# Four-layer graph network on one core: one more head's score sum on VectorE, one fewer on ScalarE, in the third layer

## The chip, the cores and the metric

The kernel runs on one core of one Trainium2 chip. The metric is the time of one execution on the device in microseconds; a version's time is the median of its runs.

## The reference

A graph has 3125 nodes with 64 features each and 103125 edges, sorted by destination (50000 drawn edges in both directions and one self loop per node). Four graph layers follow one another, each on `relu(layernorm(x))`, and each result is added to `x`: a mean aggregation (L0, two steps), a stochastic convolution (L1, two steps), a GATv2 attention with five heads (L2, two steps and a dense layer), and a relational attention (L3, two steps). Only L2 matters here. One step of it is

```
xl = (x @ Wl + bl).reshape(n, H, C);  xr = (x @ Wr + br).reshape(n, H, C)     # H = 5, C = 64
e = leaky_relu(xl[src] + xr[dst], 0.2)
alpha = einsum('ehc,hc->eh', e, att)                  # one score for each edge and head
a = exp(alpha - segment_max(alpha, dst)[dst])
out = segment_sum(a / denom[dst] * xl[src], dst)      # then the mean over heads, and a bias
```

In L2 the reference adds a self loop for each node to the edges.

## The kernel before, in words

The 103125 edges are cut into 806 tiles of 128 edges, one edge on each partition. In L2 a chunk is 18 tiles (`CT2`), so that there are 45 chunks a step, and the two steps (the loop over `l` at line 958, called "layers" of the stage below) go through all of them one after the other. Tiles are scored in pairs: 403 pairs a step, 806 in the stage.

Every table row holds 66 numbers for each head: the 64 features and two columns with 0.2 times the attention product and its negative. With these the leaky ReLU's score becomes a plain sum over 66 numbers of `max(v, 0) * weight`. For one pair `score` (line 968) does this:

- POOL gathers the source rows of 6 tiles at a time into a buffer `g` (line 976, helper at line 257; nine such buffers).
- PE makes the destination rows of each tile by a matmul of a 0/1 matrix with a window of the table (line 983), into one of two PSUM tiles `px`.
- VectorE adds both (line 984) and applies maximum and weight (line 986), in place in `g`.
- The sums over 66 numbers give the scores `al`. `ACT_HEADS = 4` (line 862) divides them: VectorE sums the first `H - ACT_HEADS` heads of both tiles by one reduction (line 987). ScalarE sums each other head of each tile by a copy activation into a scratch tile `junk` with an accumulated output (line 991). In the profile each of these is an ACTIVATE and an ACTIVATION_READ_ACCUMULATOR.
- `top` (line 1000), called in the next pair's `score`, takes on VectorE the maximum of `al` and the self loop's score, into `am`. It needs all five sums of the pair.

The steps for a whole chunk, `weigh_turn` to `nodes`, are issued between pairs a fixed number of pairs after the chunk's last one (the list at line 1097, carried out by `attend`, line 1102): transposes of `am` on PE, scans on VectorE for the maximum of each destination, the exponential on ScalarE (line 1017), weights on VectorE (lines 1029 to 1032), the sums on PE (helper at line 254), copies from PSUM on ScalarE (lines 1047 and 1058), and the nodes' new rows. In the first step the nodes' rows are also multiplied out and stored for the second (`row_steps`, lines 904 to 945). A buffer `g` comes free when its sums on PE are done.

The text above gives the program's order. The order on each engine is drawn up when the program is built, by a planner with its own costs: of what it expects to be ready it takes the earliest of the program. Each engine then runs its list in order and waits on semaphores. Only a few instructions are pinned to the program's order (`tc.keep_in_program_order`: register loads and line 852 in L2); lines 984 to 1000 are not among them. SP issues the direct transfers, POOL the gathers.

Of the kernel before, what the change touches and what calls it, by code (L numbers as in the profile page):

```python
# [63 lines left out]
def bcast(ap, axis, n):  # L64
    shape = list(ap.shape)
    shape.insert(axis, n)
    return ap.unsqueeze(axis).to_broadcast(shape)
# [73 lines left out]
def sorted_path(ctx: ExitStack, tc: tile.TileContext, A: dict, out: bass.AP):  # L141
# [712 lines left out]
    def layer2(y_prev):  # L854
# [4 lines left out]
        GW = SW + D + 1  # L859
        MS = D + 1 + H  # L860
        GT = 6
        ACT_HEADS = 4
        t_l = [tables[f"l2_{l}l"] for l in range(2)]
        t_r = [tables[f"l2_{l}r"] for l in range(2)]
        y = tables["l2_y"]
        with tc.tile_pool(name="l2", bufs=1) as lp, tc.tile_pool(name="l2_s", bufs=2) as sp, \
# [91 lines left out]
            for l in range(2):  # L958
# [9 lines left out]
                def score(s, i):  # L968
# [15 lines left out]
                    nc.vector.tensor_add(g[:, :, :SW], g[:, :, :SW], px[:, :, :SW])  # L984
                    HV = H - ACT_HEADS
                    nc.vector.scalar_tensor_tensor(g[:, :, :F], g[:, :, :F], 0.0, bcast(att08[l], 1, 2), op0=OP.max, op1=OP.mult)  # L986
# [356 lines left out]

    y1 = spmm_layers()
    y2 = layer2(y1)
    y3 = layer3(y2)
    with tc.tile_pool(name="fin", bufs=1) as fp:
# [662 lines left out]
```

## Time and profile before

| | |
|---|---|
| median of 11 runs | 9907.65 us (9843.82 to 9937.45) |
| the profiled execution: its own time, its span | 9917.3 us, 9915.4 us |
| busy in the span: PE, DVE, ACT, POOL | 4455.0, 4240.1, 2481.6, 4957.7 us |
| L2: first and last start of line 984 | 4093.9 and 7269.8 us |
| line 984, 986, 987 on DVE (806 each), mean of one | 842, 834, 278 ns |
| line 991 on ACT (6448), mean of ACTIVATE, of the accumulator's read | 247, 187 ns |
| gathers of L2 on POOL (806 in each step), mean of one | 1116, 1100 ns |

DVE is VectorE, ACT is ScalarE, PE is TensorE, POOL is GpSimd, SP is SyncE. A row of waits reads: engine, tile and line that stood idle, what released it, the idle time in us, how often, and the longest. A row of a group ends with the busy time and the mean of one in ns, and the idle time ahead of it. A row of the timeline starts with the start and the duration in us; the idle time ahead of the instruction stands in brackets. Releasers are inferred from semaphores: "issue" means that nothing visible was waited for, "remote" an unknown queue. Both instructions of a sum on ScalarE overlap the next one's, so that their durations add up to more than the engine's busy time.

### The profile page before, as it was taken

To read this page: it belongs to the slowest core of one execution; us is meant where nothing else is said; L and a number is where in the kernel's file an instruction comes from. 1 tells how busy PE (TensorE), PEld (TensorE's weight loads), DVE (VectorE), ACT (ScalarE), POOL (GpSimd) and SP (SyncE) were. 2 spreads that over 40 slices of the span, in tenths; PEclk is the share of its full clock that TensorE was granted. 3 is DMA by queue.
4 is the path that set the end of the run, shared out by engine and by line. 5 is a ranking of instruction groups with operands and counts; after the bars stand their busy time and mean duration, and the time that the engine had idled before them with its cause. 6 is when DMAs were issued, how large, how long until landed. Compare 5 with 4: busy or idle time off the path is not lost. (4 is left out here: it accounts for less than half of the span.)

```text
span 9915.4 us, 104742 instructions
## 1 busy us (share of the span) xinstructions
PE 4455.0 (45%) x23937; PEld 3412.8 (34%) x23937; DVE 4240.1 (43%) x12144; ACT 2481.6 (25%) x15657; POOL 4957.7 (50%) x4849
## 2 busy tenths in 40 slices
PE   5996995322222223355555434444452333422222
PEld 5995994222222222122222212222232222312222
DVE  5762111212212223577777757666642333323333
ACT  2331000000000000366666546555530000100000
POOL 0000003666666665255656455555526666566665
PEclk8996555555655666555555555555555555555555
DMA  2332332111111121344454344444421222111111
GB/s 70 125 118 80 136 131 67 46 47 46 47 43 46 46 50 43 119 128 134 136 137 137 108 123 123 127 119 127 121 68 37 42 41 42 40 32 35 35 35 35
DMA packets 542968, 799.05 MB, mean 81 GB/s; under 512 B 253426, under 2 KB 386153, under 8 KB 530315
## 3 DMA queue, kind: packets, MB, share of 16 engines
q0 software_dynamic: 206464, 439.52, 18.4%
q1 hardware_dynamic: 335883, 352.72, 11.3%
q8 instruction: 209, 3.42, 0.2%
q14 instruction: 412, 3.38, 0.1%
HBM read 657.39 MB, written 134.39 MB: 80 GB/s over the span
## 5 line engine op out<-in xcount | busy, mean ns | idle before, releaser
L257 POOL DMA_INDIRECT g<-l,idx x1616 | 1568.2, 970 | 2330.2 <-issue 2022.3
L991 ACT ACTIVATE junk<-g 128x66 f32<-128x66 f32 x6448 | 1573.9, 247 | 877.5 <-ACT junk L991 375.1
L257 POOL DMA_INDIRECT g<-l_0l,src_t x806 | 899.3, 1116 | 786.9 <-PE px L983 257.6
L257 POOL DMA_INDIRECT g<-l_1l,src_t x806 | 886.8, 1100 | 746.8 <-PE acc L254 404.5
L991 ACT ACTIVATION_READ_ACCUMULATOR junk<-g 128x1 f32 x6448 | 1207.3, 187 | 0.2
L257 POOL DMA_INDIRECT g<-l_0v,idx x806 | 795.0, 986 | 575.3 <-issue 216.7
L257 POOL DMA_INDIRECT g<-l_1v,idx x806 | 806.4, 1001 | 436.5 <-issue 232.9
L537 PE MATMUL acc<-hit,g 128*128 128x128 f32 x3232 | 624.3, 355 | 815.7 <-issue 476.4
L983 PE MATMUL px<-win,oT 36*128 36x335 bf16 x1612 | 569.5, 461 | 646.4 <-DVE g L984 439.1
L537 PEld LDWEIGHTS acc<-hit,g 128*128 128x128 f32 x3232 | 561.5, 260 | 863.0 <-issue 510.3
L984 DVE TENSOR_TENSOR g<-g,px 128x670 f32<-128x670 f32 x806 | 667.7, 842 | 373.5 <-remote 178.1
L612 PE MATMUL pv<-h_l,a 128*128 128x64 f32 x4700 | 800.9, 347 | 15.8 <-ACT a L605 13.4
L612 PEld LDWEIGHTS pv<-h_l,a 128*128 128x128 f32 x4700 | 792.2, 262 | 43.8 <-ACT a L605 28.3
L986 DVE SCALAR_TENSOR_TENSOR g<-g,att 128x660 f32<-128x660 f32 x806 | 670.5, 834 | 0.0
L254 PE MATMUL acc<-ao,g 128*70 128x72 f32 x3224 | 444.2, 329 | 276.4 <-DVE ao L1032 159.6
L254 PEld LDWEIGHTS acc<-ao,g 128*70 128x70 f32 x3224 | 401.0, 236 | 405.2 <-DVE ao L1032 239.3
L540 ACT COPY sums<-acc 128x128 f32<-128x128 f32 x68 | 18.1, 266 | 2056.6 <-remote 1413.3
L254 PE MATMUL acc<-oh,g 128*68 128x12 f32 x3224 | 400.2, 268 | 210.2 <-issue 102.6
L245 DVE TENSOR_TENSOR sums<-sums,carry 128x1 f32<-128x1 f32 (+2 forms) x166 | 26.0, 157 | 1079.0 <-issue 718.6
L822 PE MATMUL pm<-ident,mx 90*128 90x90 f32 (+2 forms) x158 | 65.3, 413 | 932.1 <-DVE mx L820 621.9
L1257 ACT COPY qm<-px 128x128 f32<-128x128 f32 x404 | 104.5, 267 | 1469.4 <-remote 787.2
L254 PEld LDWEIGHTS acc<-oh,g 128*68 128x68 f32 x3224 | 382.0, 230 | 249.8 <-issue 122.7
(327 smaller groups left out, 7505.9 us busy)
## 6 DMA issues: line engine op xcount, KB each, us to landing
a_d<-a SPq DMA_DIRECT2D x47, 1600.0 KB
a<-a_d SPq DMA_DIRECT2D x47, 1600.0 KB
g<-l,idx POOLq DMA_INDIRECT x1616
ea<-in_edge_attr_dram SPq DMA_DIRECT2D x33, 768.0 KB
ea<-in_edge_attr_n_dram SPq DMA_DIRECT2D x33, 768.0 KB
oT<-dl_d SPq DMA_DIRECT2D x88, 162.0 KB
oT<-dl_d SPq DMA_DIRECT2D x66, 216.0 KB
g<-l_0l,src_t POOLq DMA_INDIRECT x806
```

What stands on the lines that cost most here:

```text
L245: return tc.keep_in_program_order(op(*args, **kwargs))
L254: nc.tensor.matmul(acc[..., bass.ds(at, width)], lhsT, rhs, start=False, stop=True, skip_group_check=True)
L257: nc.gpsimd.indirect_dma_start(out=to, out_offset=None, in_=table, in_offset=bass.IndirectOffsetOnAxis(ap=idx, axis=0))
L537: nc.tensor.matmul(st["acc"][:M], g[:, k, :], h[:, k, :], start=(i == 0 and k == 0), stop=(end and k == 3))
L540: nc.scalar.copy(st["sums"][:M], st["acc"][:M])
L612: nc.tensor.matmul(st["pv"][:, :D], st["a"][:, b], h_l[l][:, b], start=(b == 0), stop=(b == NBK - 1))
L822: nc.tensor.transpose(s["pm"][:, :R], m[:R], ident[:R, :R])
L983: nc.tensor.matmul(px[:, j, :SW], s["oT"][:, q * P:(q + 1) * P], s["win"][:, i, :], start=True, stop=True)
L984: nc.vector.tensor_add(g[:, :, :SW], g[:, :, :SW], px[:, :, :SW])
L986: nc.vector.scalar_tensor_tensor(g[:, :, :F], g[:, :, :F], 0.0, bcast(att08[l], 1, 2), op0=OP.max, op1=OP.mult)
L991: nc.scalar.activation(junk, g[:, j, hd * C2:(hd + 1) * C2], AF.Copy, accum_out=al[:, q0 + j, hd:hd + 1])
L1257: nc.scalar.copy(qm[:, :m].rearrange("p k h r -> p (k h r)"), px[:, :m * H * R])
```

## The change

`ACT_HEADS` goes from 4 to 3. `HV` in `score` becomes 2, and with it line 987 reduces 128 x (2 tiles, 2 heads, 66) in place of 128 x (2 tiles, 1 head, 66), and the loop at line 989 issues three activations for each tile in place of four, six for a pair in place of eight. Nothing else of the source changes; the planner draws up the order anew.

```
         MS = D + 1 + H
         GT = 6
-        ACT_HEADS = 4
+        ACT_HEADS = 3
         t_l = [tables[f"l2_{l}l"] for l in range(2)]
...
                    HV = H - ACT_HEADS
                    nc.vector.scalar_tensor_tensor(g[:, :, :F], g[:, :, :F], 0.0, bcast(att08[l], 1, 2), op0=OP.max, op1=OP.mult)
                    nc.vector.tensor_reduce(al[:, q0:q0 + 2, :HV], g[:, :, :HV * C2].rearrange("p k (h c) -> p k h c", h=HV), AX.X, OP.add)
                    for j in range(2):
                        for hd in range(HV, H):
                            junk = sp.tile([P, C2], F32, name="junk")
                            nc.scalar.activation(junk, g[:, j, hd * C2:(hd + 1) * C2], AF.Copy,
                                                 accum_out=al[:, q0 + j, hd:hd + 1])
```

More of the change, by code (lines that the diff above doesn't have):

```diff
@@ L861, in layer2 @@
         GT = 6
-        ACT_HEADS = 4
+        ACT_HEADS = 3
         t_l = [tables[f"l2_{l}l"] for l in range(2)]
```

## The prediction

> **What bounds the kernel now.** I read the page's busy line and its 40 slices first, to see that no engine is full over the whole span, and then only the stage that the change touches. Line 984 runs in that stage alone, from 4093.9 to 7269.8 us in the view of that line: 3176 us, 806 pairs of tiles, 3.94 us a pair. The busy time by stretch, one row for each of the two layers of the stage (PE, weight loads, DVE, ACT, POOL), says:
>
> ```profile
> 4090.00:5665.00 1575.00, 763.22 (x3458) 428.71 (x3458) 1171.15 (x3206) 946.96 (x6755) 893.29 (x802) 0.52 0.48 130
> 5700.00:7250.00 1550.00, 683.31 (x3226) 393.88 (x3226) 1014.50 (x2751) 883.45 (x6440) 873.76 (x793) 0.51 0.45 123
> ```
>
> VectorE is the busiest, 74% and 65%, and nobody is full. The first layer also prepares the rows of the next one, which costs VectorE 157 us more, and yet both layers take nearly the same time. So VectorE's sum of work is not what sets the pace. The waits of VectorE in the stage say what does:
>
> ```profile
> DVE am L1000 <- ACT junk L991: 396.9, 174, 9.5
> DVE g L984 <- remote: 178.1, 19, 16.8
> DVE am L1000 <- remote: 104.0, 15, 20.0
> DVE g L984 <- PE px L983: 97.9, 64, 2.7
> DVE g L984 <- issue: 53.3, 30, 7.9
> DVE am L1000 <- issue: 44.8, 15, 20.7
> ```
>
> The largest one is line 1000, the maximum over the scores, waiting for ScalarE's sums of line 991. Going through all 806 of them, 221 sit behind a gap of more than 0.1 us, 572 us together. The reader should compare that with the load: ScalarE is busy 60% of the time, so it is late, not full. Why it is late shows in the order of time; here are one of these waits and ScalarE's activations ahead of it:
>
> ```profile
> 6199.19 0.26 ACT L991 ACTIVATE junk<-g 128x66 f32<-128x66 f32 x1 [1.08 <-ACT junk L991]
> 6200.62 0.26 ACT L991 ACTIVATE junk<-g 128x66 f32<-128x66 f32 x1 [1.08 <-ACT junk L991]
> 6202.04 0.26 ACT L991 ACTIVATE junk<-g 128x66 f32<-128x66 f32 x1 [1.06 <-ACT junk L991]
> 6203.46 0.26 ACT L991 ACTIVATE junk<-g 128x66 f32<-128x66 f32 x1 [1.07 <-ACT junk L991]
> 6204.89 0.26 ACT L991 ACTIVATE junk<-g 128x66 f32<-128x66 f32 x1 [1.07 <-issue]
> 6206.97 0.26 ACT L991 ACTIVATE junk<-g 128x66 f32<-128x66 f32 x1 [1.74 <-remote]
> 6207.69 0.26 ACT L991 ACTIVATE junk<-g 128x66 f32<-128x66 f32 x1 [0.37 <-ACT junk L991]
> 6207.95 0.24 ACT L991 ACTIVATE junk<-g 128x66 f32<-128x66 f32 x1
> 6208.19 0.24 ACT L991 ACTIVATE junk<-g 128x66 f32<-128x66 f32 x1
> ...
> 6207.69 0.17 DVE L1000 TENSOR_TENSOR am<-al,g 128x10 f32<-128x10 f32 x1 [8.84 <-ACT junk L991]
> ```
>
> Undisturbed, an activation with its read of the accumulator starts every 0.24 us (the last rows). In stretches it starts only every 1.42 us, though it has its data. Such stretches lie where POOL has been sending gathers back to back; ScalarE runs at full pace when POOL pauses. The eight activations of a pair take 1.70 us from the first start to the last in the median; 131 of the 806 groups take over 3 us, 742 us together. I don't know what slows them; what matters here is that the price is paid per activation.
>
> **The change, part by part.** *Removed:* two of eight activations per pair, with their accumulator reads. At 0.24 us start to start that is 0.48 us a pair, 806 x 0.48 = 387 us of ScalarE. Where ScalarE is undisturbed this is worth almost nothing by itself: VectorE has 2.8 us of other work per pair beside it (2236 us busy from 4090 to 7300, over 806). It is worth something where line 1000 waits. For each of the 221 waits I took the start times of its eight activations. If the last two drop out and the others keep their times, the wait gets shorter by the time from the sixth start to the eighth, at most by the whole wait: 256 us together. If instead a quarter of the group's length goes, again at most the wait, it is 217 us. I take 217, because the activations that leave are the fourth and the eighth, not the last two.
>
> *Added:* line 987 sums 264 elements in place of 132. The rows near it:
>
> ```profile
> L987 DVE TENSOR_REDUCE al<-g 128x2 f32<-128x132 f32 x288 | 77.9, 279 | 0.0
> L936 DVE TENSOR_REDUCE xr<-es 85x5 f32<-85x330 f32 x32 | 15.5, 485 | 0.0
> L1073 DVE TENSOR_REDUCE hn<-num 85x64 f32<-85x320 f32 x32 | 21.3, 665 | 0.0
> ```
>
> Lines 987 and 936 read along the row: (485 - 279) / (330 - 132) = 1.04 ns an element, so 132 more elements cost 0.138 us, 111 us over 806 pairs. Line 1073 reads across heads, 2.1 ns an element; by it the sum would be up to 0.27 us a pair, 220 us, the upper end. The new sum reads along the row, so I take 0.138. In the 221 pairs that wait at line 1000 the longer sum runs inside the wait, since ScalarE's activations need line 986 and not line 987; that leaves 585 x 0.138 = 81 us. The lower end is nothing, by the two layers above: 157 us more of VectorE's work did not lengthen a layer, and the addition is 55 us a layer.
>
> *Neither adds nor moves:* transfers. The gathers, the window loads and the register loads on SP are the same. POOL waits for ScalarE's reads of the gathered buffers (152 us in its waits), and would get buffers no later; the gather of a pair ends some 30 us before line 984 reads it (the pair at 4638.5 us was gathered by 4596.5), so that is cover enough for a late buffer. PE's line 983 waits 439 us for line 984 to free one of two banks; the 0.14 us reaches PE there, and comes back to line 984 only where PE is late, 98 us in line 984's waits. No wait is added; what gets done earlier is what stands behind the activations on ScalarE, its copies for PE (lines 1047, 1058), and no transfer hangs on those alone.
>
> *Sum:* 81 - 217 = -136 us if the slow stretches shrink with the number of activations. But the stretches follow POOL's gathers, whose number stays. If the 742 us stay as they are, groups of six pass through them faster: 131 x 8 / 6 = 175 pairs in place of 131, 44 more. A pair outside costs (3176 - 742) / 675 = 3.61 us, so that is 44 x 3.61 = 159 us gained, less 81: -78 us. I take -85, near the second, because ScalarE's pace follows the gathers in the rows. The profiled execution took 9917.3 us (span 9915.4), 9.65 us above the median of the 11 runs, so the sum is carried to the median: 9907.65 - 85 = 9823 us.
>
> A rule against this: the Trainium skill, Perfetto Trace Analysis, section Identifying the Most-Contended Engine, says to find the engine with the highest occupancy and to improve that one first. By it VectorE is the engine to relieve, the change loads it further, and the time would rise by up to the whole 111 us, to 10019. The wait rows say that the busiest engine stands still for the less busy one, and the comparison of the layers agrees with the rows; so I go by them.
>
> **The rivals.**
> *VectorE is on the path after all (slower).* In the undisturbed stretches VectorE's instructions follow one another without a gap, and any addition there goes to the end. If the time lost in the slow stretches does not fall (ScalarE's lateness then being a matter of the stretch alone, with the same 572 us of waits), the change costs 81 to 111 us: 9989 to 10019. For it: the first layer has the more work and the fewer long gaps. Against it: the equal length of the layers, and waits that end with a particular activation. It decides if less than 81 us of the 572 disappear.
> *The order is drawn up anew and line 1000 comes earlier (slower).* No wait pins line 1000 among VectorE's instructions; it stands where the planner expects ScalarE to be done. With six activations it can move ahead of one more of the long steps, line 984 or 986, 0.84 us each. In an undisturbed stretch that costs nothing; at a wait, that step no longer runs before it. 221 x 0.84 = 186 us at most, against the 136 gained: +50, 9958. It decides from 162 waits that lose a step. Against it: the gap in the order between lines 986 and 987 of the next pair, where line 1000 often stands now, is already early.
> *The gain is taken elsewhere (no change).* The long gaps at line 984 (178 us, 19 times, in the second layer nearly all) can grow by what those at line 1000 lose, as POOL waits 405 us in that layer for PE's sums (line 254) to free buffers. Then the first layer gains its half of the 85, and the second only pays its half of the 81: 9907.65 - 42 + 41 = 9906.
>
> **How the numbers follow.** Within 0.3% (30 us) is about what a measurement can't tell from no change. The forecast, faster by more than that: 0.50; it spans from 9690 (256 gained at line 1000 and a quarter of the 178 at line 984, 81 paid) to 9875. No change: 0.13. VectorE on the path: 0.19. Order: 0.18. So faster 0.50, same 0.13, slower 0.37. The range of 9690 to 10005 leaves out about one in ten on each side: a costlier sum or both slower cases together above, a collapse of the slow stretches below.
>
> **What would show it.** Right: line 987 at about 416 ns over 264 elements, 806 times; line 991 at 4836, still 0.24 us apart when undisturbed; line 1000's gaps 100 to 220 us below 572; the last start of line 984 some 85 us earlier against the first; VectorE's busy time 111 us up. Wrong: the gaps at line 1000 as long as before (first rival), more but shorter gaps there with line 984 now behind them (second), or growing gaps at line 984 and in POOL's waits for PE (third). What would make it wrong most simply is that the pace of the activations in the slow stretches depends on how many there are, in either direction.

## The result and the profile after

The changed kernel takes 10156.3 us (median of 12 runs, 10138 to 10197) against 9892.8 us (46 runs of the kernel before): ratio 1.0269, 95% interval 1.0252 to 1.0286. It is slower by 263 us, where 85 us less had been predicted. Its profiled execution took 10160.05 us with a span of 10158.3 us.

By the first and last start of line 984, the stage of L2 splits like this:

| us | before | after | difference |
|---|---|---|---|
| first step of L2 | 1553.4 | 1832.9 | +279.5 |
| between the steps | 42.7 | 43.1 | +0.4 |
| second step of L2 | 1579.9 | 1535.9 | -44.0 |
| after the last line 984 | 2645.6 | 2657.2 | +11.6 |

One step of L2 gained 44 us, and the other lost 280. Here is the busy time of the two steps after the change (columns as in the prediction: PE, weight loads, DVE, ACT, POOL):

```profile
4090.00:5940.00 1850.00, 797.27 (x3454) 440.07 (x3455) 1222.18 (x3206) 743.84 (x5143) 845.58 (x798) 0.50 0.41 111
5965.00:7500.00 1535.00, 689.45 (x3301) 392.82 (x3300) 1119.43 (x2813) 704.95 (x4978) 855.31 (x801) 0.51 0.46 125
```

In the first step nobody works much more than before, and VectorE is now busy 66% of it instead of 74%. So the loss is waiting. The groups of lines 991, 987 and 1000 in the stage say that the instructions themselves came out as predicted (busy time, mean ns of one, idle time ahead):

```profile
L991 ACT ACTIVATE junk<-g 128x66 f32<-128x66 f32 x4836 | 1183.8, 247 | 1179.1 <-issue 604.8 <-ACT junk L991 318.7 <-remote 176.9
L987 DVE TENSOR_REDUCE al<-g 128x4 f32<-128x264 f32 x806 | 328.7, 417 | 0.0
L1000 DVE TENSOR_TENSOR am<-al,g 128x10 f32<-128x10 f32 x806 | 135.0, 167 | 366.9 <-ACT junk L991 267.0 <-remote 71.0 <-issue 23.4
```

The wait at line 1000 shrank, 572 to 367 us, but in the first step alone: counting gaps of more than 0.1 us, it went from 283 to 73 us there, and from 288 to 290 in the second. The waits of VectorE in the stage show what took its place, and those of ScalarE where it comes from:

```profile
DVE am L1000 <- ACT junk L991: 267.0, 158, 6.4
DVE g L984 <- PE px L983: 248.7, 95, 12.8
DVE g L984 <- remote: 178.6, 35, 13.9
DVE g L984 <- PE pt L810: 143.1, 16, 10.8
```

```profile
ACT junk L991 <- issue: 604.8, 324, 11.3
ACT junk L991 <- ACT junk L991: 318.7, 502, 1.6
ACT sums L1047 <- remote: 224.2, 50, 13.3
ACT u L1058 <- remote: 204.7, 30, 8.7
```

VectorE now stands ahead of line 984. Counted in the same way, the gaps there went from 116 to 554 us in the first step. That rise of 437 us, less the 210 at line 1000, plus the 51 us by which VectorE's work grew, is 278 of the step's 279.5. In the second step the gaps at line 984 went the other way, 257 to 129 us; that is where its gain comes from. And ScalarE has two new waits that end with nothing visible: the copy `sums` (line 1047) and the copy `u` (line 1058). The next rows are one chunk's end in the first step, ScalarE, PE and VectorE in three fences (start, duration, and idle time in brackets):

```profile
5581.49 0.58 ACT L1047 COPY sums<-acc 70x510 f32<-70x510 f32 x1 [2.63 <-remote]
5588.66 0.43 ACT L1058 COPY u<-px 85x330 f32<-85x330 f32 x1 [6.59 <-remote]
```

```profile
5582.13 1.70 PE L1055 MATMUL px<-wh,sums 70*85 70x65 f32 x10 [2.46 <-issue]
5583.62 0.39 PE L1056 MATMUL px<-wsel,sums 70*85 70x5 f32 x2
5583.94 0.74 PE L983 MATMUL px<-win,oT 36*128 36x335 bf16 x2
...
5589.15 0.72 PE L983 MATMUL px<-win,oT 36*128 36x335 bf16 x2 [3.90 <-ACT u L1058]
```

```profile
5581.96 0.22 DVE L1138 COPY am<-am 128x5 f32<-128x5 f32 x1
5590.77 0.85 DVE L984 TENSOR_TENSOR g<-g,px 128x670 f32<-128x670 f32 x1 [8.59 <-PE pt L810]
...
5595.70 0.85 DVE L984 TENSOR_TENSOR g<-g,px 128x670 f32<-128x670 f32 x1 [3.99 <-remote]
```

PE has `px` ready for the copy at 5584.01 (5583.62 + 0.39). ScalarE has nothing else to do and starts the copy at 5588.66, 4.65 us late. `u` is read from one of the two `px` tiles, so PE's line 983 at 5589.15 waits for it. VectorE stands still ahead of line 984 for 8.59 us, and for 3.99 more one pair later, and only a part of this is a wait for that tile. The pair that starts at 5590.77 had its `px`, the other tile, at 5584.68 (5583.94 + 0.74), and the next one, at 5595.70, had its own at 5589.87 (5589.15 + 0.72). So VectorE, too, starts some 6 us late with its data there. Going through the first step by pairs, 59 of its lines 984 that wait for PE's semaphore alone start over 0.5 us after their `px` was done and VectorE was free, 290 of the 554 us; in the kernel before these are 2 in the first step (7 us) and 26 in the second (134 us). `u` is late like this in 31 of the step's chunks. The same place in the kernel before, at the end of a chunk of the first step:

```profile
4683.77 0.58 ACT L1047 COPY sums<-acc 70x510 f32<-70x510 f32 x1 [1.56 <-PE acc L1044]
4686.32 0.43 ACT L1058 COPY u<-px 85x330 f32<-85x330 f32 x1 [1.97 <-PE px L1056]
```

There the copy follows its matmul at once. In the kernel before, gathers go out around the copies too, but one at `sums` takes 2.51 us, and behind it the run begins anew:

```profile
4682.49 2.51 POOL L257 DMA_INDIRECT g<-l_0l,src_t  x1 [0.30 <-issue]
4685.31 0.94 POOL L257 DMA_INDIRECT g<-l_0l,src_t  x1 [0.30 <-issue]
```

After the change, gathers run back to back, 1.25 us apart, all through the late copies, having started 11 us ahead of `sums` (with a long one at 5573.20, so that by the count of runs used below this one starts at 5575.86):

```profile
5570.42 1.18 POOL L257 DMA_INDIRECT g<-l_0l,src_t  x1 [18.60 <-PE acc L254]
...
5587.49 0.94 POOL L257 DMA_INDIRECT g<-l_0l,src_t  x1 [0.30 <-issue]
5588.74 0.94 POOL L257 DMA_INDIRECT g<-l_0l,src_t  x1 [0.30 <-issue]
```

This run of gathers was released by PE's sums (line 254), which read the buffers. So I compared PE's order. In the first step the kernel before has, at a chunk's end, one part of the sums (12 matmuls), two pairs of line 983, and then two parts together (24 matmuls), line 1044 and the copy `sums`. After the change the planner put two pairs of line 983 between the second and the third part as well. In the traces' medians the three parts end 7.5, 2.5 and 1.0 us ahead of `sums` before, and 12.1, 8.4 and 2.7 us ahead of it after. The longest gather run near the copy (gathers with under 1.7 us from one to the next) starts 2.0 us after `sums` before (10 gathers), and 6.4 us ahead of it after (15 gathers). The slow stretch that the prediction describes was, before, on ordinary activations behind the copies; now it is on the copies, and on the lines 984 beside them.

**Theory A**: in long runs of gathers ScalarE issues slowly. The new order of PE's sums frees buffers earlier, the run starts ahead of the copies `sums` and `u`, and the stretch falls on these instead of on activations. **Theory B**: VectorE's longer sums are the loss. **Theory C**: VectorE's own changed order at the chunk's end is.

### The profile page after: what moved, and what is told of

It reads as the page before. It is cut to its first block, busy times and chain, and to the rows that moved or that the text cites. A ratio compares the mean times of both kernels' runs of the same rounds, so it can differ in the third digit from the quotient of the medians.

```text
span 10158.3 us, 102008 instructions
## 1 busy us (share of the span) xinstructions
PE 4499.5 (44%) x23937; PEld 3430.5 (34%) x23937; DVE 4372.8 (43%) x12144; ACT 2079.8 (20%) x12433; POOL 4893.8 (48%) x4849
## 5 line engine op out<-in xcount | busy, mean ns | idle before, releaser
L991 ACT ACTIVATE junk<-g 128x66 f32<-128x66 f32 x4836 | 1183.8, 247 | 1179.1 <-issue 604.8
L257 POOL DMA_INDIRECT g<-l_0l,src_t x806 | 855.5, 1061 | 1101.5 <-PE acc L254 689.3
L257 POOL DMA_INDIRECT g<-l_1l,src_t x806 | 860.9, 1068 | 726.4 <-ACT junk L991 392.5
L991 ACT ACTIVATION_READ_ACCUMULATOR junk<-g 128x1 f32 x4836 | 904.1, 187 | 0.0
L983 PE MATMUL px<-win,oT 36*128 36x335 bf16 x1612 | 592.7, 466 | 625.0 <-issue 306.9
L822 PEld LDWEIGHTS pm<-ident,mx 90*128 90x128 f32 (+2 forms) x158 | 28.9, 183 | 1205.6 <-DVE mx L820 773.9
```

The costliest lines, as they stand in the source:

```text
L257: nc.gpsimd.indirect_dma_start(out=to, out_offset=None, in_=table, in_offset=bass.IndirectOffsetOnAxis(ap=idx, axis=0))
L822: nc.tensor.transpose(s["pm"][:, :R], m[:R], ident[:R, :R])
L983: nc.tensor.matmul(px[:, j, :SW], s["oT"][:, q * P:(q + 1) * P], s["win"][:, i, :], start=True, stop=True)
L991: nc.scalar.activation(junk, g[:, j, hd * C2:(hd + 1) * C2], AF.Copy, accum_out=al[:, q0 + j, hd:hd + 1])
```

## The experiments

The executions below come from several groups, and each ratio is to the kernel before on the same chip in the same group. The kernel before took 10032, 10019 and 9882 us in the first three groups, and 8662 and 8663 us in the last two; that difference turns out to be the clue. The steps come from one profiled execution of each version, and the groups differ in level (four heads in the first step take 1642 us in heads3_step2 and 1553 in the kernel before), so small differences of steps across groups say nothing. "Long" counts the gathers of a step, of 806, that stand in runs of 8 or more with under 1.7 us from one to the next. "Late" counts the chunks in which `u` starts more than 3 us after PE has its `px` ready (of some 44 in a step). Each pair is first step / second step.

| version | ratio (95%) | steps, us | long | late |
|---|---|---|---|---|
| before | 1 | 1553 / 1580 | 406 / 484 | 1 / 16 |
| after | 1.0269 (1.0252, 1.0286) | 1833 / 1536 | 620 / 492 | 31 / 0 |
| heads3_step2 | 1.0003 (0.9989, 1.0017) | 1642 / 1615 | 453 / 548 | 1 / 0 |
| heads3_step1 | 1.0289 (1.0261, 1.0317) | 1920 / 1574 | 672 / 459 | 40 / 19 |
| own_bank_3 | 1.0243 (1.0205, 1.0281) | 1899 / 1588 | 643 / 486 | 31 / 2 |
| own_bank_4 | 0.9873 (0.9845, 0.9901) | 1580 / 1519 | 363 / 432 | 1 / 18 |
| together_3 | 1.0040 (1.0021, 1.0059) | 1646 / 1641 | 505 / 630 | 0 / 0 |
| early_4 | 1.0439 (1.0419, 1.0459) | 1932 / 1728 | 588 / 588 | 42 / 25 |
| dve_two_act_four | 1.0536 (1.0515, 1.0558) | 1939 / 1831 | 454 / 502 | 39 / 1 |
| dve_one_act_three | 1.0211 (1.0191, 1.0231) | 1885 / 1517 | 493 / 596 | 40 / 0 |
| spread_3 | 0.9766 (0.9725, 0.9806) | 1436 / 1440 | 61 / 425 | 0 / 0 |
| spread_4 | 0.9673 (0.9634, 0.9713) | 1445 / 1322 | 71 / 62 | 0 / 0 |
| own_together_3 | 0.9782 (0.9738, 0.9826) | 1481 / 1392 | 258 / 250 | 2 / 3 |
| no_gather_3 | 0.9390 (0.9353, 0.9426) | 1323 / 1169 | none | 0 / 0 |
| no_gather_4 | 1.0001 (0.9992, 1.0011) | 1263 / 1205 | none | 0 / 0 |
| own_spread_4 | 1.0046 (1.0029, 1.0062) | 1329 / 1183 | 137 / 286 | 0 / 0 |
| own_spread_3 | 1.0089 (1.0072, 1.0106) | 1355 / 1190 | 94 / 555 | 0 / 0 |
| wide_3 | 1.0156 (1.0139, 1.0173) | 1344 / 1251 | 95 / 342 | 0 / 0 |
| after_again | 1.0026 (1.0015, 1.0037) | 1327 / 1162 | 487 / 622 | 0 / 0 |
| own_spread_4_again | 1.0049 (1.0032, 1.0066) | 1329 / 1189 | 150 / 230 | 0 / 0 |

### The change in one step alone

```
-        ACT_HEADS = 4
+        ACT_HEADS = (4, 3)          # heads3_step2; (3, 4) in heads3_step1
-                    HV = H - ACT_HEADS
+                    HV = H - ACT_HEADS[l]
```

> Three heads on ScalarE in the second step of L2 only, four in the first. Theory A (the late copy: in the first step of the changed kernel a long run of gathers starts before ScalarE's copy sums, the slow stretch falls between the copies sums and u, the heads' product holds one of the two px tiles until u is done, and PE and VectorE stand still): the first step takes 1553 us as before, the second 1536 as in the changed kernel, 44 us less than before, so about 9850 us, 0.996 of before. Theory B (VectorE's longer sums and whatever hangs on them cost in both steps): half of the 264 us, about 10025 us, 1.013.

> Three heads on ScalarE in the first step of L2 only, four in the second. Theory A: the first step takes 1833 us as in the changed kernel, with gaps of 8 to 11 us ahead of line 984 once a chunk, the second about 1580, so about 10173 us, 1.028 of before. Theory B: half of the 264 us, about 10025 us, 1.013.

The whole loss is the first step's: 1.0289 with three heads there alone, 1.0003 with three heads in the second alone. The second step's gain of the changed kernel doesn't show in the time of heads3_step2, for which theory A had 0.996. The work of VectorE and ScalarE on a pair is the same in both steps, so what is lost isn't the price of the work. In heads3_step1 PE's order at the chunk's end is that of the changed kernel, with the third part of the sums set apart, and `u` is late in 40 chunks.

### The copy's tile

`u` gets a PSUM bank of its own, so that a late copy no longer holds one of line 983's two `px` tiles. The bank is won by putting `pm` into the rest of `pt`.

```
-        s["pt"] = ps.tile([P, 3 * P], F32, name="pt")
+        s["pt"] = ps.tile([P, (4 if wide else 3) * P], F32, name="pt")
...
-        s["pm"] = ps.tile([P, P], F32, name="pm")
+        s["pm"] = pt[:, 3 * P:] if wide else ps.tile([P, P], F32, name="pm")
...
-                    pn = psx.tile([P, 2, 512], F32, name="px")[:N2, 0, :H * C1 + H]
+                    pn = ps.tile([P, 512], F32, name="pn")[:N2, :H * C1 + H]
```

> The changed kernel, with the heads' product (line 1053) in a PSUM tile of its own, so that it never holds one of the two px tiles; the room comes from putting the transposed maxima pm behind pt in one bank. Theory A: the gaps ahead of line 984 in the first step (554 us) fall below 250 us, some of them come back as waits of line 1000 for the activations queued behind the copy u; 150 to 300 us less than the changed kernel, 9850 to 10010 us, 0.996 to 1.012 of before. Theory B: px is not what matters, as the changed kernel, 10156 us, 1.027.

> The kernel before, with the same tile of its own for the heads' product. Theory A: the second step of the kernel before has the same gap in every other chunk (17 times about 11 us ahead of line 984); they shrink, 80 to 170 us less, 9720 to 9810 us, 0.983 to 0.992 of before. Theory B: no change beyond 0.3%, 9893 us.

With three heads the tile was not the coupling that matters: 1.0243. `u` is as late as before, and VectorE's wait moved back from line 984 (554 to 176 us in the first step) to line 1000 (73 to 517 us). These are its waits in own_bank_3, from 3840 to 7650 us, and the ones of ScalarE behind them:

```profile
DVE am L1000 <- ACT junk L991: 811.3, 197, 14.1
DVE g L984 <- remote: 98.3, 46, 10.1
```

```profile
ACT u L1058 <- remote: 365.4, 31, 13.6
```

Whatever stands in ScalarE's list behind the held copy is held too, activations among them. The half of theory A that made `px` the path fell here, which fits the pairs that started late with their `px` done; the half about the stretch stayed. With four heads the same edit gains 1.3%.

### When the parts of the sums are due

The three parts of PE's sums are due 7, 8 and 9 pairs after a chunk's last one. In together_3 (three heads) all are due at 9, so that none frees its buffers early; in early_4 (four heads, the kernel before in all else) two are due at 7.

```
-  (7, gather_sums(0)), (8, gather_sums(1)), (9, gather_sums(2)),
+  (9, gather_sums(0)), (9, gather_sums(1)), (9, gather_sums(2)),      # together_3
+  (7, gather_sums(0)), (7, gather_sums(1)), (9, gather_sums(2)),      # early_4
```

> The changed kernel, with the three parts of a chunk's sums on PE (gather_sums) all due 9 pairs after the chunk in place of 7, 8 and 9. On PE the order around them in the first step is then that of the kernel before (six matmuls of line 983, one part, four, two parts, then the copy sums). Theory A (revised: own_bank_3 showed that px isn't needed for the loss; what matters is that a long run of gathers starts about 6 us ahead of sums, so that the slow stretch holds the copy u and every activation behind it): the run starts at sums again, u follows within 3 us, the first step falls from 1833 to about 1560 us, the whole to 0.985 to 1.005 of before. Theory B (VectorE's longer sums): the load is the same as in the changed kernel, 1.02 to 1.03. Theory C (the changed order of VectorE's own instructions at the chunk's end, which stays): 1.02 to 1.03.

> The kernel before (four heads on ScalarE), with the parts of a chunk's sums on PE due 7, 7 and 9 pairs after the chunk in place of 7, 8 and 9, so that two of three buffers come free some two pairs ahead of the copy sums. Theory A: the run of gathers starts ahead of sums, the slow stretch falls on sums and u as in the changed kernel, and the first step gets longer by 100 to 280 us, 1.010 to 1.028 of before. Theory B and C: VectorE has the same work in nearly the same order, 0.995 to 1.005.

Both go as theory A has it, in both directions. With three heads and the second and third part together again ahead of line 1044 (in half of the chunks in the order that the kernel before has, in the others with all three parts together), the loss falls from 2.7% to 0.4%, with no late `u`. With four heads and the sums early, `u` is late in 42 chunks of the first step and the kernel loses 4.4%, without any change of the heads.

### VectorE's and ScalarE's parts of the change, each alone

dve_two_act_four sums two heads on VectorE and still runs all four activations on ScalarE, the first of them into a number that nobody reads. dve_one_act_three leaves the second head's scores at zero: VectorE sums one head, ScalarE three.

```
-  nc.vector.tensor_reduce(al[:, q0:q0 + 2, :HV], g[:, :, :HV * C2]...                 # dve_two_act_four
+  nc.vector.tensor_reduce(al[:, q0:q0 + 2, :2], g[:, :, :2 * C2]...
-      accum_out=al[:, q0 + j, hd:hd + 1])
+      accum_out=al[:, q0 + j, hd:hd + 1] if hd > 1 else spare)
...
-                        for hd in range(HV, H):                                       # dve_one_act_three
+                        for hd in range(2, H):
```

> The kernel before, with VectorE's sums over two heads as in the changed kernel, and still four activations a tile on ScalarE (the one for the second head sums into a spare tile): VectorE's part of the change alone. Theory A: on PE two parts of the sums come four and three pairs ahead of the copy sums, the third at it; the run of 12 gathers ends about at sums and u follows 16 activations later, so nothing is held that wasn't before, and the longer sums cost at most their 111 us: 1.000 to 1.011 of before. Theory B: most of the loss is here, 1.015 to 1.027.

> The kernel before, with three activations a tile on ScalarE as in the changed kernel, and VectorE still summing one head: ScalarE's part of the change alone. The second head's scores are left at zero, so one head's attention isn't computed. Theory A: PE's parts of the sums come as in the kernel with VectorE's part alone, and u follows sums directly; with the run of 12 gathers ending about at sums, 0.98 to 1.00 of before; above 1.01 if u is held all the same. Theory B: without the longer sums only the gain is left, 0.98 to 0.99.

Without VectorE's longer sums 2.1% are still lost, so most of the loss doesn't need them, against theory B. What they add can't be read from the difference to 2.7%: the two parts lose 5.4 and 2.1% alone and 2.7% together, so they don't add up. PE's order in this version has the third part of the sums apart as well (three pairs of line 983 ahead of it), and `u` is late in 40 chunks.

dve_two_act_four went far past what was expected. Its second step lost too, by another copy. Here `sums` itself is held, by more than 3 us in 41 chunks of that step; the longest gather run starts 17 us ahead of it. ScalarE's waits in its stage:

```profile
ACT junk L992 <- issue: 603.0, 309, 11.4
ACT sums L1048 <- remote: 480.9, 64, 12.1
```

PE's order in that step, at the chunk's end, is that of the kernel before and of the changed one, which lost nothing there. So the order of the sums alone doesn't decide. Nor does the start of the run: in the second step of the kernel before it is 1.1 us behind `sums`, with 16 late `u`, and in the changed kernel 2.8 us ahead of it, with none. What the stretch falls on decides, and I can't derive that from the program. With the stretch on a copy that PE waits for, each edit of work is buried under it.

### The sums spread out

If long gather runs are the root, the parts should come further apart, so that each frees one buffer and no run gets long.

```
-  (7, gather_sums(0)), (8, gather_sums(1)), (9, gather_sums(2)), (11, heads), (13, nodes)] + [(14 + i, f) ...
+  (7, gather_sums(0)), (10, gather_sums(1)), (13, gather_sums(2)), (15, heads), (17, nodes)] + [(18 + i, f) ...
```

> The changed kernel, with the three parts of PE's sums (gather_sums) due 7, 10 and 13 pairs after the chunk's last one, and heads, nodes and what follows moved back with them (15, 17, from 18). Buffers then come free apart, so that POOL should have shorter runs of back-to-back gathers. Theory A (a long gather run that starts ahead of the copies sums and u costs the loss): copy u follows the copy sums in 3 us or so in most chunks of the first step (6.5 us in the changed kernel), the first step takes 1540 to 1650 us instead of 1833, the ratio to the kernel before is 0.985 to 1.005. Theory B (VectorE's longer sums or its own order are the loss): 1.02 to 1.03, as the changed kernel.

> The kernel before (four heads on ScalarE) with the same due times, 7, 10 and 13, then 15, 17, from 18. Theory A: the kernel before has its own share of late copies in the second step (u 4.3 us after sums in the median), which goes too: 0.985 to 1.000, and the difference to the run with three heads is then what the change is worth with the order of the sums held alike: three heads 0 to 0.8% faster. Theory B: three heads 1 to 3% slower than this run.

Both gain more than expected, and spread_4 beats both kernels by 3.3% and more. The expectation that `u` follows `sums` in 3 us was wrong for spread_3 (10.2 us): there PE's matmul itself comes later, waiting for line 984 to free a `px`, and that costs little. What counts is the time from the matmul to the copy, and by that no chunk is late. Three heads are 1.0% slower than four, where theory A had them up to 0.8% faster and theory B 1 to 3% slower. Where both versions have short runs, in the first step, they take the same time (1436 and 1445 us). The 1% is all in the second step, where only the version with three heads still has 425 gathers in long runs. That fits theory A; it isn't isolated.

### Both, and no gathers

own_together_3 puts the bank of its own and the due times of together_3 on the changed kernel. no_gather_3 replaces the gathers of L2 in the changed kernel:

```
-                        for k in range(min(GT, n - q0)):
-                            t = c * CT2 + q0 + k
-                            gather(s["g"][-1][:, k, :GW], t_l[l], by_tile["src"][:, t:t + 1])
+                        m = min(GT, n - q0)
+                        nc.sync.dma_start(s["g"][-1][:, :m, :GW], t_l[l][:m * P].rearrange("(k p) f -> p k f", p=P))
```

> The changed kernel with the nodes' numbers in a PSUM bank of their own (no longer one of the two px tiles) and the three parts of PE's sums all due 9 pairs after the chunk's last one. With four heads the bank alone gave 0.987; with three heads the due times alone 1.004, the bank alone 1.024. Theory A: both together take the late copies away and the coupling with px as well: 0.985 to 0.997, first step 1540 to 1620 us. Theory B (VectorE's longer sums): not below 1.01.

> The changed kernel without the gathers of the third layer: each buffer of 6 tiles is filled by one plain transfer of 768 consecutive table rows from SP's queue, so the rows are not gathered by source and the scores are those of other edges; all other work stays, and POOL issues no gathers there. Theory A in its strong form (ScalarE's slow stretches come with POOL's runs of gathers): line 991 starts every 0.24 to 0.3 us throughout, copy u follows the copy sums in 2 to 3 us in both steps, a step takes 1250 to 1500 us, the ratio is 0.90 to 0.96. If the slow stretches belong to ScalarE's activations or to the arrival of data and not to POOL's gathers: they stay, with steps of 1500 to 1830 us, 0.99 to 1.03.

own_together_3 gives 0.978, below the band that was expected, with half as many gathers in long runs. Without gathers the two steps take 1323 and 1169 us where the changed kernel took 1833 and 1536: on a chip with the stretches, 877 us of the stage exist only with the gathers, though a pair's gathers ended some 30 us ahead of its line 984 in the prediction's row. VectorE's waits in its stage:

```profile
DVE g L983 <- PE px L982: 140.1, 119, 11.2
DVE am L999 <- ACT junk L990: 38.7, 100, 1.2
```

(This file is a line shorter: its 983 is line 984, its 999 line 1000.) The wait at line 1000, 572 us in the kernel before, is 39.

### A group in which the stretches are missing

Open was then what the change is worth by itself: VectorE's sums or the second step's runs. no_gather_4 is the kernel before without gathers, own_spread_3 and own_spread_4 combine the bank and the spread, and wide_3 spreads the changed kernel's sums further.

```
+  (7, gather_sums(0)), (11, gather_sums(1)), (15, gather_sums(2)), (17, heads), (19, nodes)] + [(20 + i, f) ...    # wide_3
```

> The kernel before (four heads on ScalarE) without the gathers of the third layer, as in the run no_gather_3: plain transfers of consecutive rows in their place, so the scores are those of other edges. Three heads gave 0.939. Theory A (the change loses only by the order of the sums against the gathers): equal within 0.4%, 0.935 to 0.943. Theory B (VectorE's longer sums cost by themselves): 111 us by the prediction's price, so 0.925 to 0.930.

> Four heads, parts of PE's sums due 7, 10, 13 and the nodes' numbers in a bank of their own. The due times alone gave 0.967, the bank alone 0.987. Nodes' matmuls waited 113 us for line 984 to free px with the due times alone; without that wait 0.955 to 0.967.

> The same with three heads. With the due times alone the nodes' matmuls waited 212 us for line 984 to free px, and the second step kept long gather runs. Theory A: where the runs are short (under 150 of 806 gathers in runs of 8 or more) a step is within 1.5% of the one of own_spread_4, and the ratio is 0.955 to 0.970. Theory B: 50 us or more slower in each step than own_spread_4, whatever the runs.

> Three heads, parts of PE's sums due 7, 11 and 15 pairs after the chunk's last one (heads 17, nodes 19, then from 20). Theory A: fewer gathers in long runs in the second step than the 425 with 7, 10, 13, and that step shorter than 1440 us; ratio 0.960 to 0.975. Theory B: no better than 0.977. Buffers that are held longer can make POOL late instead: above 0.985.

All four came out outside what theory A, or its prices, had for them, and for one reason: in this group the kernel before took 8662 us. Leaving the gathers out gains nothing (1.0001), and the versions with spread sums, where spread_4 had gained 3.3%, lose 0.5 to 1.6%. The traces show why. Taking line 991's starts between the seventh and the last gather of a run, the median step to the next start and its upper quartile are 0.71 and 1.41 us in the kernel before, 0.58 and 1.39 in the changed one, 1.43 and 2.80 in spread_4 (70 starts only); in own_spread_4 and own_spread_3 both are 0.24. POOL gathers at the same 1.25 us in all of them. The stretches are not there.

The changed kernel itself, and own_spread_4 once more:

> The changed kernel itself once more. Theory A (the loss is ScalarE's slow stretch falling on the copies sums and u): if activations behind the seventh gather of a run start 0.24 us apart in the median, as on the last chip, 1.000 to 1.010, with copy u within 3.5 us of sums in the first step; if they start 0.3 us apart or more, 1.02 to 1.03 again, with u some 6 us behind. Theory B (the new order or VectorE's sums cost by themselves): 1.02 to 1.03 on either kind of chip.

> Four heads, parts of PE's sums due 7, 10, 13, nodes' numbers in a bank of their own, as in own_spread_4. Theory A: 0.950 to 0.968 where the slow stretches exist (the due times alone gave 0.967, the bank alone 0.987), 1.003 to 1.006 as before where they do not. If the gain of the spread was not that of shorter gather runs: the same ratio on both kinds of chip.

The stretches were missing again (0.24 us in the median and the upper quartile of the changed kernel), and both came out as theory A has it for that case: 1.0026 and 1.0049. The changed kernel has as many long runs as any (487 and 622 gathers of 806), the program is the one that lost 2.7%, and the copies pass through the run unharmed. ScalarE and POOL in after_again, at one chunk's end of the first step:

```profile
4619.59 0.58 ACT L1047 COPY sums<-acc 70x510 f32<-70x510 f32 x1 [0.84 <-PE acc L1044]
4622.15 0.43 ACT L1058 COPY u<-px 85x330 f32<-85x330 f32 x1 [1.97 <-PE px L1056]
4622.48 0.26 ACT L991 ACTIVATE junk<-g 128x66 f32<-128x66 f32 x1
```

```profile
4610.23 1.18 POOL L257 DMA_INDIRECT g<-l_0l,src_t  x1 [3.33 <-PE acc L254]
...
4619.50 0.95 POOL L257 DMA_INDIRECT g<-l_0l,src_t  x1 [0.30 <-issue]
4620.75 1.33 POOL L257 DMA_INDIRECT g<-l_0l,src_t  x1 [0.30 <-DMA g<-l_0l,src_t]
4622.38 0.94 POOL L257 DMA_INDIRECT g<-l_0l,src_t  x1 [0.30 <-issue]
4623.63 0.95 POOL L257 DMA_INDIRECT g<-l_0l,src_t  x1 [0.30 <-issue]
```

The run started 9 us ahead of `sums`, as in the slow case, and `u` starts at 4622.15, 2.56 us behind `sums`. VectorE isn't held either. The next rows are the pair at the place in its chunk that the pair of 5590.77 has, with its `px` on PE and its line 984:

```profile
4622.04 0.74 PE L983 MATMUL px<-win,oT 36*128 36x335 bf16 x2
```

```profile
4622.81 0.85 DVE L984 TENSOR_TENSOR g<-g,px 128x670 f32<-128x670 f32 x1 [0.74 <-PE px L983]
```

No line 984 that waits for PE's semaphore alone starts over 0.5 us late in after_again, nor in no_gather_3. Theories B and C by themselves are worth no more than the 0.26% here, for VectorE's sums and its order are those of the changed kernel. Its steps take 1327 and 1162 us, against 1323 and 1169 without gathers in no_gather_3, on a chip that had the stretches. That is the strongest row of the study: take the stretches away in either manner, and the changed kernel's steps come to within 0.7% of the same times.

What the change is worth by itself follows from there: +0.26% (23 us of 8663) in after_again, and own_spread_3 against own_spread_4, 8741.8 to 8707.4, +0.40% (34 us). It is a small loss. VectorE is then nearly full:

```profile
3850.00:5176.00 1326.00, 780.20 (x3386) 427.52 (x3384) 1207.61 (x3154) 722.36 (x5115) 929.95 (x798) 0.50 0.57 154
5219.00:6381.00 1162.00, 676.93 (x3302) 386.75 (x3300) 1109.37 (x2815) 667.82 (x4985) 876.72 (x801) 0.51 0.61 165
```

These are the two steps of after_again: VectorE works 91% and 95% of them.

No version is known to gain on both kinds of execution. spread_4 is the best where the stretches exist (0.967); without them it wasn't run, and its sibling own_spread_4 costs 0.5% there.

## Why the prediction was wrong

**Prices right, two more signs by luck.** Line 987 takes 417 ns over 264 elements (416 forecast), line 991 comes 4836 times and still 0.24 us apart when undisturbed. VectorE's busy time in the whole execution rose from 4240.1 to 4372.8 us, 133 (111 forecast). The waits at line 1000 fell by 205 us, inside the 100 to 220, and the second step gained 44 us, which is half of the 85. Neither is the forecast mechanism. The fall is all in the first step, the one that lost, where the time came back ahead of line 984. In the second step line 1000 waits as before (288 and 290 us); the gain is at line 984, 257 to 129 us, and goes with the late `u`, 16 before and none after. So no run shows the 159 or the 217 us that the sum gave to fewer activations: where the stretches are missing, the change loses 0.26%. Of the signs that it listed, two spoke against it: the last start of line 984 came 236 us later against the first, not 85 earlier, and the gaps at line 984 grew.

**The step that failed: "Neither adds nor moves: transfers", with the line that POOL "would get buffers no later".** It asked whether the gathers could be late, found 30 us of cover, and put nothing into the sum for the order between engines. They became early. The planner, drawing up the order anew, set the parts of PE's sums apart in the first step; buffers came free earlier, and the run of gathers, whose slow stretch the prediction had itself described, started ahead of the copies `sums` and `u` instead of behind them. The text says of these copies that no transfer hangs on them alone. True, but PE's next pair hangs on `u`, through the `px` tile, and the activations of the next pairs hang on it in ScalarE's list; and VectorE's line 984 is held beside them. together_3 and early_4 show the cause in both directions, after_again that it needs the stretches.

**The price of a stretch was put "per activation".** Its price is set by the instruction it falls on. On line 991 it was 572 us of waits over both steps, with the remaining work beside it; on the copies and the lines 984 beside them it is 8.6 us and some 4 more, in most chunks. Of the 333 us between forecast and result, 322 are the first step's: +279.5 measured where half of -85 was due.

**The rivals.** *VectorE on the path*: its condition was that less than 81 of the 572 us disappear; 205 did, and the loss came all the same, 2.1% of it without the longer sums. Where the stretches are missing it does become the bound, at 23 to 34 us instead of 81 to 111. *The order drawn up anew* was the right word in the wrong place: it looked at line 1000 on VectorE alone and priced it at +50; what mattered was the order on PE and what it releases on POOL. *The gain taken elsewhere* named line 984, and its gaps did grow, 373 to 683 us in both steps; but in the first step, not the second. POOL's waits for PE's sums grew there too, 36 to 689 us, as that rival's sign has it; but no gather came late by them, for line 984 waits 3 us in all for one.

**The rule weighed.** The Trainium skill, Perfetto Trace Analysis, section Identifying the Most-Contended Engine, would have had the busiest engine, VectorE, relieved and not loaded. The sign came out as it says. Where the stretches exist its reason isn't the one that the runs show. Where they are missing, VectorE works 91% and 95% of the two steps, and there the rule holds, with a loss of 0.3 to 0.4%.

**The range** (9690 to 10005) left out the result, because every case in it moved one engine's work and none the order between two engines.

## What to carry to other kernels

Where a program's order is drawn up anew, compare the orders on all engines, those that the change doesn't touch too, and ask what they release earlier, not only what may come late. A stretch in which an engine starts its instructions late is priced by the instruction that it falls on: find the few instructions there that another engine waits for. And when a loss is traced to such a stretch, look at whether it exists in every execution: an edit that dodges it can gain 3% in one place and lose 0.5% in another.

## What the runs showed of the hardware

While POOL issues indirect gathers back to back (1.25 us apart), ScalarE starts its next instruction only some 0.7 or 1.4 us later instead of 0.24, above all behind a run's seventh gather: in the kernel before the upper quartile from one activation to the next is 1.41 us there, and 0.26 us behind the first six. Copies wait as activations do (`u` 4.65 us after its matmul in the rows above). VectorE is held too where it waits for another engine, by up to 9.6 us ahead of line 984 in the changed kernel. Where it waits for nothing but its own semaphore it never stands over 0.3 us, in 3267 instructions of L2 in that kernel, and PE's line 1055 starts 0.05 us after `sums` has ended in all 90 chunks.

So the stretches look less like slow issue than like waits whose end comes late. In the changed kernel's trace, updates of PE's semaphore are recorded at 5588.64 and at 5590.75, each 0.02 us ahead of the late `u` and the late line 984, and none between 5581.47 and 5588.64, though matmuls that update it ended at 5584.01 and 5584.68. Of the 72 late lines 984 of both steps, 90% start within 0.06 us of a recorded update of PE's semaphore. The records themselves differ: of the updates that PE, VectorE and ScalarE make in L2, the traces hold 66 to 81% in both kernels of the result and in every version of the first three groups that gathers in L2, 99% or more in those of the last two groups, and all of them in no_gather_3 and no_gather_4. The runs don't show whether the update, its arrival or the matmul's end was late.

This was there in the profiled executions of both kernels and in the first three groups of runs, and not in the last two, where the kernel before takes 8662 us instead of 9882 to 10032: 12 to 14% less for the same program. Not all of it lies in L2: in after_again 2306 us follow the last line 984 instead of 2657, and its first start comes at 3849 us instead of 4089. The gathers' own spacing, 1.25 us, is the same in both. Two groups that carry the same chip number had the stretches and had them not, so the runs don't settle whether it is a matter of the chip or of the time. What delays the waits isn't known either: no row shows a resource that the engines share with the gathers.
